# Second layer's first 18 chunks gathered from a table without its last two blocks, those two added by counted products

## The chip, the cores and the metric

The kernel runs on one core of one Trainium2 chip. The metric is device time in microseconds (us) of one execution; a kernel's time is the median of its runs. TensorE is called PE here, VectorE DVE, ScalarE ACT, GpSimd POOL and SyncE SP, as the profile does. POOL and SP also issue transfers (DMAs); an indirect DMA of POOL, a gather, fetches 128 rows of a table by 128 row numbers.

## The reference, cut to what matters

The kernel computes two layers of a graph network over 6250 nodes of 512 numbers and 100,000 edges, which come sorted by `dst`.

```python
norm = -dinv[src] * dinv[dst]                    # dinv: 1/sqrt(degree by src)

def cheb_conv(x, W0, W1, b):
    tx1 = segment_sum(x[src] * norm[:, None], dst, num_segments=N)
    return x @ W0 + tx1 @ W1 + b

h = maximum(layernorm(x), 0)
h = cheb_conv(h, W1_0, W1_1, b1)
h = layer_norm(h) * gamma + beta
h = where(h >= 0, h, 0.01 * h)
out = x + cheb_conv(h, W2_0, W2_1, b2)
```

Both layers need, for each edge, the row of its source node, added up at its target node. The second layer's rows are the first layer's output.

## The kernel before

**Units of work.** The nodes are cut into 49 blocks of 128 rows (the last has 106), the edges into 782 chunks of 128. Three chunks make a unit, four units a group: 66 groups, the first of which has one unit (chunks 0 to 2), so that group 1 has chunks 3 to 14 and group 2 chunks 15 to 26. Layer 0 and layer 1 (the code counts from 0) run the same loop over the groups, the last loop of `usual_path`.

**Tables.** For each layer a table in DRAM holds the rows that the edges fetch. `tab[0]` is made from `x` at the start. `tab[1]` is written by layer 0, block by block, in `finish` (L565), with a copy of the layer's plain output in `h_tab` (L570).

**Gathers.** `gather_to` issues one indirect DMA on POOL for each chunk (L386): the 128 rows named by column `t` of `sidx` go to one of 57 places in `places`, in a ring, so chunk `t` takes the place that chunk `t - 57` had. A gather waits until PE has used the old chunk; a gather from `tab[1]` also waits for the writes of the rows that it reads. At the top of each group gathers are issued 57 chunks ahead of its first chunk.

**Sums.** `choose` makes on DVE a matrix of zeros and ones for each unit (`sel`, L505), which says which of the unit's 32 target nodes each edge of a chunk belongs to. `sums` multiplies the gathered rows by it (L517), and ACT copies the result to `agg` (L520). `place` moves the groups' sums to the rows of a block by another matrix of zeros and ones, `there` (L530, L532).

**Blocks.** When a block's last group is done, `turn` transposes the block's own rows (L456) and places its sums (L582), and `dense` transposes these (L589), copies them back (`aT`, L591) and makes the products with the two weights (L468). `finish` then does the layer norm on DVE and ACT (L549 to L559), makes the scaled row `t` for `tab[1]` (L562, L563) and `g` for `h_tab` (L567, L568), and SP stores both. The own products of blocks 46, 47 and 48 are made ahead (`EARLY`, tiles `pre`), since these blocks come last. Layer 0's group 64 finishes block 46 ahead of its sums, and blocks 47 and 48 follow after groups 64 and 65.

**Order.** `usual_path` takes the order of PE, POOL and SP from the source (`manual_schedule`). The order of DVE and ACT is made by the scheduler of the framework, which also puts in the waits that the data ask for: a write waits for earlier reads of the same part of a tile. Each engine works through its instructions in order.

**Start of the program.** For its first 60 chunks layer 0 gathers from `x` itself; `look_up` finds the two numbers that each row is scaled with (tiles `is_hi` and `both`, L428 to L435), from group 3 on not any more.

Of the kernel before, what the change touches and what calls it, by code (L numbers as in the profile page):

```python
# [8 lines left out]
F32 = mybir.dt.float32  # L9
BF = mybir.dt.bfloat16  # L10
I32 = mybir.dt.int32
AF = mybir.ActivationFunctionType
OP = mybir.AluOpType
# [6 lines left out]
P = 128  # L20
# [4 lines left out]
Q = 32  # L25
# [2 lines left out]
DRIFT = 32  # L28
RE = 16
RAW = 60  # L30


def parts(r):

    return [(lo, hi) for lo, hi in ((0, r - r % 16), (r - r % 16, r)) if lo < hi]
# [3 lines left out]
def gnn_kernel(  # L39
# [33 lines left out]
    nc = tc.nc  # L73
    N, D = x.shape
    E = src.shape[0]
    NB = -(-N // P)
# [3 lines left out]
    KD = D // P  # L80
    NC = -(-E // P)
# [3 lines left out]
    NS = -(-NU // NQ)  # L85
    unit = [max(0, NU - NQ * (NS - g)) for g in range(NS + 1)]
    rows = [min(P, N - i * P) for i in range(NB)]
    LAST = 8

    const = ctx.enter_context(tc.tile_pool(name="const", bufs=1))  # L90
    dram = ctx.enter_context(tc.tile_pool(name="dram", bufs=1, space=bass.MemoryType.DRAM))
# [2 lines left out]

        return bass.AP(tensor=ap.tensor, offset=ap.offset, ap=[[0, n], [1, ap.shape[0]]])

    tab = [dram.tile([n, D], F32, name=f"tab{i}") for i, n in enumerate((NB * P, N))]
    h_tab = dram.tile([N, D], F32, name="h_tab")

    ident = const.tile([P, P], F32, name="ident")  # L100
    iota_r = const.tile([P, P], F32, name="iota_r")
# [14 lines left out]
    gam = const.tile([P, D], F32, name="gam")  # L116
    bet = const.tile([P, D], F32, name="bet")
    sidx = const.tile([P, NG * P], I32, name="sidx")
    w_sb = [const.tile([P, KD, D], F32, name=f"w{i}") for i in range(2)]
    diff = const.tile([P, P], F32, name="diff")  # L120
    sc = const.tile([P, 2, NB], F32, name="sc")
    pick = const.tile([P, P], BF, name="pick")
    src_lo = const.tile([P, P], BF, name="src_lo")
    src_hi = const.tile([P, RAW], F32, name="src_hi")
    p_id = const.tile([P, 1], F32, name="p_id")
# [4 lines left out]
    places = stay.enter_context(tc.tile_pool(name="places", bufs=1)).tile([P, NB + RE, D], F32, name="places")  # L130
    w_at = NB - 2 * KD
    order = list(range(NB, NB + RE)) + list(range(w_at))
# [31 lines left out]
    groups, i = [], 0  # L164
# [4 lines left out]
    xs = []  # L169
# [11 lines left out]
        xs.append(t)  # L181
    for t, w in zip(w_sb, (W1_1, W1_0)):
        nc.sync.dma_start(t, w.rearrange("(k p) d -> p k d", p=P))
    for t, v in ((bias1, b1), (bias2, b2), (gam, gamma), (bet, beta)):
        nc.sync.dma_start(t, dup(v, P))

# [166 lines left out]
def usual_path(tc, have):  # L353
    nc = tc.nc
    (x, out, tab, h_tab, ndinv, sidx, dlx, iota_r, w_sb, W2_1, W2_0, w_late, ident, eps, ones, first, nodes_ps, node_of, minus,
     unsorted, ln, dinv, sdinv, bias1, bias2, gam, bet, unseen, unit, N, E, D, NB, NC, NU, NS, KD, rows, places, order,
     groups, xs, sc, pick, src_lo, src_hi, p_id) = (
        have[n] for n in ("x out tab h_tab ndinv sidx dlx iota_r w_sb W2_1 W2_0 w_late ident eps ones first nodes_ps node_of "
                          "minus unsorted ln dinv sdinv bias1 bias2 gam bet unseen unit N E D NB NC NU NS KD rows places "
                          "order groups xs sc pick src_lo src_hi p_id").split())  # L360
    AHEAD = 2
    EARLY = {NB - 3: NS - 11, NB - 2: NS - 9, NB - 1: NS - 7}
    ACT = mybir.EngineType.Activation
# [9 lines left out]
    with ExitStack() as es:  # L373
# [1 line left out]
        psum = es.enter_context(tc.tile_pool(name="main_ps", bufs=2, space=bass.MemoryType.PSUM))  # L375
        es.enter_context(tc.manual_schedule(engines={PE, POOL, SP}))
        is_lo, found, looked, gathered = [], 0, 0, RE
        own_h, own_x, agg, placed, started, pre = {}, {}, {}, {}, {}, {}

        def zr(t):  # L380
            return places[:, order[t % R], :]

        def gather_to(layer, end):
            nonlocal gathered
            for t in range(gathered, min(end, NC)):
                nc.gpsimd.indirect_dma_start(  # L386
                    out=zr(t), out_offset=None, in_=x if layer == 0 and t < RAW else tab[layer],
                    in_offset=bass.IndirectOffsetOnAxis(ap=sidx[:, t : t + 1], axis=0))
            gathered = max(gathered, min(end, NC))

        def make_table(g, engines):

# [24 lines left out]
        def look_up(tag):  # L417
            nonlocal looked
            if looked == RAW:
                return  # L420
            at_lo = psum.tile([P, 4, P], F32, name=tag)
            at = looked
            assert at + 4 <= gathered
            where = is_lo.pop(0)
            for j in range(4):
                nc.tensor.matmul(at_lo[:, j, : 2 * NB], where[:, j, :], sc.rearrange("p k b -> p (k b)"),  # L426
                                 start=True, stop=True)
            is_hi = pool.tile([P, 4, NB], F32, name="is_hi", bufs=1)  # L428
            nc.vector.tensor_tensor(is_hi, src_hi[:, at : at + 4, None].to_broadcast([P, 4, NB]),
                                    iota_r[:, None, :NB].to_broadcast([P, 4, NB]), op=OP.is_equal)  # L430
            both = pool.tile([P, 4, 2, NB], F32, name="both", bufs=1)
            nc.vector.tensor_tensor(both, at_lo[:, :, : 2 * NB].rearrange("p j (k b) -> p j k b", k=2),
                                    is_hi[:, :, None, :].to_broadcast([P, 4, 2, NB]), op=OP.mult)
            ac = pool.tile([P, 4, 2], F32, name="ac", bufs=4)
            nc.vector.tensor_reduce(ac, both, AX.X, OP.add)  # L435
            for j in range(4):
                nc.scalar.activation(zr(at + j), zr(at + j), AF.Relu, bias=ac[:, j, 1:2], scale=ac[:, j, 0:1])
            looked += 4
# [32 lines left out]
        def load_early(layer, i):  # L471
            load_h(layer, i, "pre", len(EARLY))
            pre[i] = own_h[i]
            if layer == 1:
                load_x(i)

# [29 lines left out]
                                            node[:, q : q + k, None, :].to_broadcast([P, k, w, Q]), op=OP.is_equal)  # L506
            return sel, chunk

        def sums(g, sel, chunk):

            n = len(chunk)
            ps = psum.tile([P, D], F32, name="ps")
            todo = [(s, q) for s in range(STEP) for q in range(n) if s < len(chunk[q])]
            if g == NS - 1:
                todo.sort(key=lambda t: chunk[t[1]][t[0]])
            for s, q in todo:
                nc.tensor.matmul(ps[q * Q : (q + 1) * Q, :], sel[:, q, s, :], zr(chunk[q][s]), start=(s == 0),  # L517
                                 stop=(s == len(chunk[q]) - 1))
            agg[g] = pool.tile([P, D], F32, name="agg", bufs=3)
            nc.scalar.activation(agg[g][: n * Q], ps[: n * Q], AF.Copy)  # L520

# [13 lines left out]
        def finish(layer, i, v):  # L535
            r = rows[i]
            v = v[:r]
            if layer == 1:
                o = pool.tile([P, D], F32, name="t")
                if i in EARLY:  # L540
                    nc.vector.tensor_add(o[:r], v, pre.pop(i)[:r])
                else:
                    nc.vector.tensor_add(v, v, bias2[:r])  # L543
                    nc.vector.tensor_add(o[:r], v, own_x.pop(i)[:r])
                for lo, hi in parts(r):
                    nc.sync.dma_start(out[i * P + lo : i * P + hi, :], o[lo:hi])
                return
            if i < NB - 1:
                nc.vector.tensor_add(v, v, pre.pop(i)[:r] if i in EARLY else bias1[:r])  # L549
            st = pool.tile([P, 6], F32, name="st")  # L550
            mv = pool.tile([P, 2], F32, name="mv")
            nc.vector.bn_stats(st[:r], v)
            nc.vector.bn_aggr(mv[:r], st[:r])
            sd = pool.tile([P, 1], F32, name="sd")
            nc.scalar.activation(sd[:r], mv[:r, 1:2], AF.Sqrt, bias=eps[:r])
            rs = pool.tile([P, 1], F32, name="rs")
            nc.vector.scalar_tensor_tensor(v, v, mv[:r, 0:1], gam[:r], op0=OP.subtract, op1=OP.mult)
            nc.vector.reciprocal(rs[:r], sd[:r])
            nc.vector.scalar_tensor_tensor(v, v, rs[:r], bet[:r], op0=OP.mult, op1=OP.add)  # L559

            t = pool.tile([P, D], F32, name="t")
            nc.scalar.activation(t[:r], v, AF.Copy, scale=sdinv[:r, i : i + 1])  # L562
            nc.vector.scalar_tensor_tensor(t[:r], v, dinv[:r, i : i + 1], t[:r], op0=OP.mult, op1=OP.max)  # L563
            for lo, hi in parts(r):
                nc.sync.dma_start(tab[1][i * P + lo : i * P + hi, :], t[lo:hi])  # L565
            g = pool.tile([P, D], F32, name="g", bufs=1)
            nc.scalar.activation(g[:r], v, AF.Copy, scale=SLOPE)  # L567
            nc.vector.tensor_tensor(g[:r], v, g[:r], op=OP.max)  # L568
            for lo, hi in parts(r):
                nc.sync.dma_start(h_tab[i * P + lo : i * P + hi, :], g[lo:hi])  # L570
# [86 lines left out]

        for layer in range(2):
            if layer == 1:
                gathered = 0  # L660
                for i in range(AHEAD):
                    load(layer, i)
            i = 0
            for g in range(NS):
# [16 lines left out]
                if g == NS - 2:  # L681
                    for k, (hT, an) in due:
                        dense(layer, k, hT, an)
                    due = []
                sums(g, *(chosen if g == NS - 1 else choose(g)))
                if layer == 0:
                    if g == 0:
                        more_tables(1, [DVE, ACT])
# [350 lines left out]
```

## Time and profile before

| | |
|---|---|
| median of 3 runs | 2095.71 us (2095.39 to 2096.01) |
| the profiled execution | 2097.45 us |
| its span, from the first to the last instruction | 2095.5 us |
| PE matmul busy | 1742.9 us, 83% of the span |
| POOL busy | 1497.7 us, 71% |
| DVE busy | 673.7 us, 32% |
| ACT busy | 444.6 us, 21% |
| DMA | 520.33 MB, mean 248 GB/s |
| mean granted clock of PE | 0.916 of full speed |

Busy time leaves out the time in which an engine issues: POOL is busy for some 0.95 us of each gather and idle for 0.30 us between two. In the timelines below a row is: start in us from the span's start, length in us, engine, line, operation, what is written and from what, how many instructions are merged in the row, and in brackets the idle time before it and what ended that. A row of the waits is: engine, tile and line that waited, for whom, us in total, times, longest.

### The profile page before, as it was taken

To read this page: it belongs to the slowest core of one execution; us is meant where nothing else is said; L and a number is where in the kernel's file an instruction comes from. 1 tells how busy PE (TensorE), PEld (TensorE's weight loads), DVE (VectorE), ACT (ScalarE), POOL (GpSimd) and SP (SyncE) were. 2 spreads that over 40 slices of the span, in tenths; PEclk is the share of its full clock that TensorE was granted. 3 is DMA by queue.
4 is the path that set the end of the run, shared out by engine and by line. 5 is a ranking of instruction groups with operands and counts; after the bars stand their busy time and mean duration, and the time that the engine had idled before them with its cause. 6 is when DMAs were issued, how large, how long until landed. Compare 5 with 4: busy or idle time off the path is not lost.

```text
span 2095.5 us, 19192 instructions
## 1 busy us (share of the span) xinstructions
PE 1742.9 (83%) x6708; PEld 662.6 (32%) x6708; DVE 673.7 (32%) x1373; ACT 444.6 (21%) x795; POOL 1497.7 (71%) x1577
## 2 busy tenths in 40 slices
PE   5568888988888889889866888988888889888997
PEld 4433323332323233323321323333223233333332
DVE  8983333333243333333340212222112112221221
ACT  8684222222122221222210101101011011010110
POOL 5067777777777777777747777777777777777774
PEclk9779989999999999989997999999999999999999
DMA  9298888787788887878757788878787788788875
GB/s 369 73 364 269 255 255 253 242 256 244 251 281 254 255 247 248 256 246 262 238 183 216 242 253 255 253 244 254 241 255 240 256 255 251 244 256 251 273 236 156
DMA packets 184793, 520.33 MB, mean 248 GB/s; under 512 B 30321, under 2 KB 31883, under 8 KB 184686
## 3 DMA queue, kind: packets, MB, share of 16 engines
q0 software_dynamic: 125120, 410.09, 64.4%
q1 hardware_dynamic: 59566, 108.91, 14.1%
q8 instruction: 55, 0.90, 0.2%
q14 instruction: 52, 0.43, 0.1%
HBM read 467.64 MB, written 51.25 MB: 248 GB/s over the span
## 4 chain that ended last, share of the span: by engine, by line
PE 40%; DMA 33%; POOL 12%; issue 9%; DVE 5%; ACT 1%; POOLq 0%; SPq 0%; ACTq 0%; DVEq 0%
DMA places<-tab,sidx 32%; PE u_ps L468 19%; POOL places L386 12%; PE ps L517 12%; PE an_ps L532 5%; PE hT_ps L589 2%; PE hT_ps L456 1%; DVE lo L254 1%; DVE hi L254 1%; PE both_ps L260 1%; PE hT_ps L426 0%; DVE places L397 0%; DVE places L398 0%; DMA h<-in_x_dram 0%; DMA places<-in_x_dram,sidx 0%
## 5 line engine op out<-in xcount | busy, mean ns | idle before, releaser
L386 POOL DMA_INDIRECT places<-tab,sidx x1504 | 1422.7, 946 | 480.7 <-issue 310.5
L517 PE MATMUL ps<-places,sel 128*32 128x512 f32 x3128 | 630.3, 706 | 256.8 <-DMA places<-tab,sidx 249.9
L517 PEld LDWEIGHTS ps<-places,sel 128*32 128x32 f32 x3128 | 116.9, 118 | 730.7 <-DMA places<-tab,sidx 506.8
L505 DVE TENSOR_TENSOR sel<-dlx,nodes_ps 128x384 f32<-128x384 f32 (+3 forms) x134 | 72.3, 541 | 656.3 <-PE ps L517 656.3
L532 PE MATMUL an_ps<-agg,there 128*128 128x512 f32 (+1 forms) x580 | 267.7, 596 | 1.5 <-ACT agg L520 1.5
L520 ACT ACTIVATE agg<-ps 128x512 f32<-128x512 f32 (+1 forms) x132 | 78.8, 597 | 809.2 <-PE ps L517 807.3
L468 PE MATMUL u_ps<-places,hT 128*128 128x512 f32 (+1 forms) x392 | 180.3, 603 | 2.2 <-ACT hT L458 2.2
L468 PE MATMUL u_ps<-w,hT 128*128 128x512 f32 (+1 forms) x392 | 178.6, 599 | 2.4 <-ACT hT L458 2.4
L468 PE MATMUL u_ps<-places,aT 128*128 128x512 f32 (+1 forms) x392 | 176.5, 593 | 2.3 <-DVE aT L591 2.3
L468 PE MATMUL u_ps<-w,aT 128*128 128x512 f32 (+1 forms) x392 | 176.5, 593 | 2.3 <-DVE aT L591 2.3
L532 PEld LDWEIGHTS an_ps<-agg,there 128*128 128x128 f32 (+1 forms) x580 | 103.2, 191 | 99.3 <-issue 88.2
L458 ACT ACTIVATE hT<-hT_ps 128x512 f32<-128x512 f32 (+1 forms) x98 | 58.2, 594 | 344.6 <-PE hT_ps L456 343.0
L543 DVE TENSOR_TENSOR u_ps<-u_ps,bias 128x512 f32<-128x512 f32 x46 | 32.2, 700 | 278.4 <-PE u_ps L468 278.4
L549 DVE TENSOR_TENSOR u_ps<-u_ps,bias 128x512 f32<-128x512 f32 x46 | 32.2, 700 | 260.1 <-PE u_ps L468 260.1
L530 DVE TENSOR_SCALAR there<-iota_r,node_of 128x128 f32<-128x128 f32 (+1 forms) x290 | 89.0, 307 | 75.8 <-PE an_ps L532 75.5
L386 POOL DMA_INDIRECT places<-in_x_dram,sidx x44 | 44.5, 1011 | 83.9 <-ACT places L400 58.2
L468 PEld LDWEIGHTS u_ps<-w,aT 128*128 128x128 f32 (+1 forms) x392 | 74.1, 190 | 95.4 <-issue 92.4
L468 PEld LDWEIGHTS u_ps<-places,aT 128*128 128x128 f32 (+1 forms) x392 | 74.1, 190 | 95.4 <-issue 92.4
L468 PEld LDWEIGHTS u_ps<-places,hT 128*128 128x128 f32 (+1 forms) x392 | 72.4, 195 | 75.5 <-issue 72.7
L582 ACT ACTIVATE an<-an_ps,ndinv 128x512 f32<-128x512 f32 (+1 forms) x98 | 67.3, 687 | 135.0 <-PE an_ps L532 135.0
L468 PEld LDWEIGHTS u_ps<-w,hT 128*128 128x128 f32 (+1 forms) x392 | 71.3, 192 | 74.7 <-issue 71.7
L591 DVE COPY aT<-hT_ps 128x512 f32<-128x512 f32 (+1 forms) x98 | 67.5, 688 | 37.9 <-PE hT_ps L589 36.2
(138 smaller groups left out, 1089.1 us busy)
## 6 DMA issues: line engine op xcount, KB each, us to landing
places<-tab,sidx POOLq DMA_INDIRECT x1504, 3.8
tab<-t SPq DMA_DIRECT2D x48, 256.0 KB, 3.9
h_tab<-g SPq DMA_DIRECT2D x48, 256.0 KB, 5.5
xt<-in_x_dram SPq DMA_DIRECT2D x48, 256.0 KB, 4.5
out_dram<-t SPq DMA_DIRECT2D x48, 256.0 KB, 4.2
h<-in_x_dram SPq DMA_DIRECT2D x46, 256.0 KB, 5.7
h<-h_tab SPq DMA_DIRECT2D x46, 256.0 KB, 4.5
tab<-places SPq DMA_DIRECT2D x5, 1792.0 KB
```

Of the source, the lines that this page charges most:

```text
L254: nc.vector.tensor_tensor(t, s[:, g * 2 * GJ : (g + 1) * 2 * GJ].rearrange("p (j s) -> p j s", s=2)[:, :, None, :] .to_broadcast([EP, GJ, ...
L386: nc.gpsimd.indirect_dma_start(out=zr(t), out_offset=None, in_=x if layer == 0 and t < RAW else tab[layer], in_offset=bass.IndirectOffsetO ...
L458: nc.scalar.activation(hT[:, :, :r], ps[:, :, :r], AF.Copy)
L468: nc.tensor.matmul(u_ps[:r], hT[:, kc, :r], w[:, kc, :], start=(start and kc == 0), stop=(stop and kc == KD - 1))
L505: nc.vector.tensor_tensor(sel[:, q : q + k, :w, :], of, node[:, q : q + k, None, :].to_broadcast([P, k, w, Q]), op=OP.is_equal)
L517: nc.tensor.matmul(ps[q * Q : (q + 1) * Q, :], sel[:, q, s, :], zr(chunk[q][s]), start=(s == 0), stop=(s == len(chunk[q]) - 1))
L520: nc.scalar.activation(agg[g][: n * Q], ps[: n * Q], AF.Copy)
L530: nc.vector.tensor_scalar(there[:m, :r], iota_r[:m, :r], node_of[:m, g : g + 1], -(1.0 + i * P), op0=OP.subtract, op1=OP.is_equal)
L532: nc.tensor.matmul(placed[i][:r], there[:m, :r], agg[g][:m, :], start=(g == inside[i][0]), stop=(g == inside[i][-1]))
L582: nc.scalar.activation(an[:r], placed.pop(i)[:r], AF.Copy, scale=ndinv[:r, i : i + 1])
L589: nc.tensor.transpose(ps[:, kc, :r], an[:r, kc * P : (kc + 1) * P], ident[:r, :r])
L591: nc.vector.tensor_copy(aT[:, :, :r], ps[:, :, :r])
```

## The change

Layer 1's chunks 0 to 17 are no longer gathered with the others but by `gather_ahead`, which layer 0's group 64 calls when block 46 is finished (`LATE = 2` blocks, `AHEAD_OF = 18` chunks). They read only `tab[1][: zero_row + 1]`, blocks 0 to 46 and one more row, `zero_row` = 47 x 128 = 6016, which holds zeros. Edges whose source is in block 47 or 48 read that zero row: `eidx` is the smaller of the source's number and 6016. Blocks 47 and 48 are stored one row further down in `tab[1]`, and `shift` adds 1 to the row numbers from 6016 on in `sidx`, in two halves: columns 0 to 511 in layer 0's group 50, columns 512 to 781 in layer 1's group 2. Layer 1's other gathers start at chunk 18 and read `sidx` as before.

What the zero row left out is added in groups 0 to 2 of layer 1. `count_late` counts on PE, for each of the two blocks, how many edges go from each of its rows to each of a unit's 32 target nodes: for each chunk and block DVE makes a mask (edge by row of the block), and PE multiplies it by `sel`. `sums` then multiplies these counts by the rows of the two blocks, which stay in SBUF: for blocks 47 and 48 `finish` writes `t` into the block's `pre` tile (`late`). That makes 36 masks, 36 matmuls of counts and 12 products of 512 columns.

To make room in SBUF, `is_hi` and `both` of `look_up` now lie in the buffers of `aT` and `g`.

```diff
+LATE = 2
+AHEAD_OF = 18
...
-    tab = [dram.tile([n, D], F32, name=f"tab{i}") for i, n in enumerate((NB * P, N))]
+    tab = [dram.tile([n, D], F32, name=f"tab{i}") for i, n in enumerate((NB * P, N + 1))]
+    zero_row = (NB - LATE) * P
...
+    eidx = const.tile([P, AHEAD_OF], I32, name="eidx")
+    e_src = const.tile([P, AHEAD_OF], F32, name="e_src")
...
+    nc.sync.dma_start(tab[1][zero_row : zero_row + 1, :], places[P - 1 : P, NB - 1, :])
...
+        def gather_ahead():
+
+            for t in range(AHEAD_OF):
+                nc.gpsimd.indirect_dma_start(
+                    out=zr(t), out_offset=None, in_=tab[1][: zero_row + 1, :],
+                    in_offset=bass.IndirectOffsetOnAxis(ap=eidx[:, t : t + 1], axis=0))
+
+        def shift(lo, hi):
+
+            at, up = (pool.tile([P, D], F32, name="xt")[:, : hi - lo] for _ in range(2))
+            nc.vector.tensor_copy(at, sidx[:, lo:hi])
+            if lo == 0:
+                nc.vector.tensor_copy(e_src, at[:, :AHEAD_OF])
+                nc.vector.tensor_scalar_min(up[:, :AHEAD_OF], at[:, :AHEAD_OF], float(zero_row))
+                nc.vector.tensor_copy(eidx, up[:, :AHEAD_OF])
+            nc.vector.tensor_single_scalar(up, at, float(zero_row), op=OP.is_ge)
+            nc.vector.tensor_add(at, at, up)
+            nc.vector.tensor_copy(sidx[:, lo:hi], at)
...
-            is_hi = pool.tile([P, 4, NB], F32, name="is_hi", bufs=1)
+            is_hi = pool.tile([P, KD, P], F32, name="aT", bufs=1)[:, :, :NB]
...
-            both = pool.tile([P, 4, 2, NB], F32, name="both", bufs=1)
+            both = pool.tile([P, D], F32, name="g", bufs=1)[:, : 8 * NB].rearrange("p (j k b) -> p j k b", j=4, k=2)
...
             pre[i] = own_h[i]
+            if layer == 0 and i >= NB - LATE:
+                late[i] = pre[i]
...
+        def count_late(sel, chunk):
+
+            some = [q for q, c in enumerate(chunk) if c[0] < AHEAD_OF]
+            if not some:
+                return None
+            ps = psum.tile([P, LATE, P], F32, name="hT_ps")
+            for q in some:
+                for b in range(LATE):
+                    for k, t in enumerate(chunk[q]):
+                        hot = pool.tile([P, P], F32, name="there", bufs=3)
+                        nc.vector.tensor_scalar(hot, iota_r, e_src[:, t : t + 1], -float(zero_row + b * P),
+                                                op0=OP.subtract, op1=OP.is_equal)
+                        nc.tensor.matmul(ps[:, b, q * Q : (q + 1) * Q], hot, sel[:, q, k, :], start=(k == 0),
+                                         stop=(k == len(chunk[q]) - 1))
+            cnt = pool.tile([P, LATE, P], F32, name="cnt", bufs=1)
+            w = len(some) * Q
+            nc.vector.tensor_copy(cnt[:, :, :w], ps[:, :, :w])
+            return cnt
...
-        def sums(g, sel, chunk):
+        def sums(g, sel, chunk, cnt=None):
...
-                                 stop=(s == len(chunk[q]) - 1))
+                                 stop=(s == len(chunk[q]) - 1 and (cnt is None or chunk[q][0] >= AHEAD_OF)))
+            for b in range(LATE if cnt is not None else 0):
+                r = rows[NB - LATE + b]
+                for q in range(n):
+                    if chunk[q][0] < AHEAD_OF:
+                        nc.tensor.matmul(ps[q * Q : (q + 1) * Q, :], cnt[:r, b, q * Q : (q + 1) * Q],
+                                         late[NB - LATE + b][:r], start=False, stop=(b == LATE - 1))
...
-            t = pool.tile([P, D], F32, name="t")
+            t = late[i] if i in late else pool.tile([P, D], F32, name="t")
...
+            at = i * P + (i in late)
             for lo, hi in parts(r):
-                nc.sync.dma_start(tab[1][i * P + lo : i * P + hi, :], t[lo:hi])
+                nc.sync.dma_start(tab[1][at + lo : at + hi, :], t[lo:hi])
...
             if layer == 1:
-                gathered = 0
+                gathered = AHEAD_OF
...
                     due = []
-                sums(g, *(chosen if g == NS - 1 else choose(g)))
+                    if layer == 0:
+                        assert i == NB - LATE and gathered == NC
+                        gather_ahead()
+                sel, chunk = chosen if g == NS - 1 else choose(g)
+                sums(g, sel, chunk, count_late(sel, chunk) if layer == 1 else None)
+                if g == (NS - 16, 2)[layer]:
+                    shift(*((0, SHIFTED), (SHIFTED, NC))[layer])
```

## The prediction, made before the changed kernel had run

> **What bounds the kernel now.** I read the totals first, then who GpSimd (POOL) waited for, then the timelines around the change of layer, one engine at a time. POOL sends one gather per chunk of 128 edges (L386). Its waits over the whole span, and its timeline where layer 0 ends:
>
> ```profile
> POOL places L386 <- issue: 315.0, 1034, 0.3
> POOL places L386 <- DMA h_tab<-g: 22.8, 1, 22.8
> ...
> 1069.82 0.94 POOL L386 DMA_INDIRECT places<-tab,sidx  x1 [0.30 <-issue]
> 1071.07 0.95 POOL L386 DMA_INDIRECT places<-tab,sidx  x1 [0.30 <-issue]
> 1094.77 0.94 POOL L386 DMA_INDIRECT places<-tab,sidx  x1 [22.75 <-DMA h_tab<-g]
> 1096.01 0.95 POOL L386 DMA_INDIRECT places<-tab,sidx  x1 [0.30 <-issue]
> ```
>
> The reader is to see 0.95 us of work and 0.30 us of idle per gather: a beat of 1.25 us, always "issue", so nothing holds POOL. Layer 1 is 782 beats from 1094.77 to 2071.22, and a fixed tail follows to 2095.5. Only one long wait breaks the beat: 22.75 us in which layer 1's first gather waits for the last table rows. Who writes those rows is on SyncE's queue:
>
> ```profile
> 1060.13 0.32 SPq L565 DMA_DIRECT2D tab<-t  x1
> ...
> 1068.07 0.32 SPq L565 DMA_DIRECT2D tab<-t  x1
> ...
> 1081.28 0.32 SPq L565 DMA_DIRECT2D tab<-t  x1
> ...
> 1091.67 0.73 SPq L565 DMA_DIRECT2D tab<-t  x2
> ```
>
> These are blocks 45, 46, 47 and 48; the last one's issue at 1091.67 lets POOL go 3.1 us later. TensorE (PE) is not the bound: between 691 and 1033 us it waits for gathers 40.9 us in total.
>
> **What I expect of each part.** In its aim the change is sound: 18 of the 782 beats (22.5 us) need only blocks 0 to 46 and fit the hole. But `shift` writes new indices into `sidx`, which the gathers read. A write of columns 0 to 511 must wait until layer 0's gather 511 has landed, one of columns 512 to 781 until its last, gather 781, has. PE, POOL and SP run in the order of the source; VectorE (DVE) and ScalarE have theirs from the scheduler. In the changed program as built the first write-back stands between L559 and L563 of block 26, and the second, which the source has in layer 1's group 2, between L563 and L568 of layer 0's block 43. In the trace of before these two places are
>
> ```profile
> 684.18 0.86 DVE L559 SCALAR_TENSOR_TENSOR u_ps<-u_ps,rs,bet 128x512 f32<-128x512 f32 x1
> 684.95 0.27 DVE L530 TENSOR_SCALAR there<-iota_r,node_of 128x128 f32<-128x128 f32 x1
> 685.80 0.75 DVE L563 SCALAR_TENSOR_TENSOR t<-u_ps,dinv,t 128x512 f32<-128x512 f32 x1 [0.57 <-ACT t L562]
> ...
> 1019.55 0.28 DVE L530 TENSOR_SCALAR there<-iota_r,node_of 128x128 f32<-128x128 f32 x1
> 1020.30 0.69 DVE L568 TENSOR_TENSOR g<-u_ps,g 128x512 f32<-128x512 f32 x1 [0.47 <-ACT g L567]
> ```
>
> and the gathers waited for are issued at 733.46 (270 beats before the last) and 1071.07. With the median landing of 3.8 us they are there at 737.3 and 1074.9: VectorE would stand still for 52 us and again for up to 55 us. That a waiting instruction holds all behind it is visible in the trace:
>
> ```profile
> 1078.02 0.69 ACT L562 ACTIVATE t<-u_ps,sdinv 128x512 f32<-128x512 f32 x1 [1.29 <-DVE u_ps L559]
> ...
> 1080.03 0.55 DVE L505 TENSOR_TENSOR sel<-dlx,nodes_ps 128x384 f32<-128x384 f32 x1 [2.05 <-PE ps L517]
> 1080.51 0.75 DVE L563 SCALAR_TENSOR_TENSOR t<-u_ps,dinv,t 128x512 f32<-128x512 f32 x1
> ```
>
> L563's input is ready at 1078.71, yet it runs only behind L505, which waits for PE. The Trainium skill says the same, and it speaks against this change (TensorE: Matmul & The Clock Gate, "Architectural detail: the array is 16× 32×32, not 1× 128×128": VectorE and ScalarE are strict first-in first-out). By that rule alone the two waits are unavoidable; the row agrees with 1.8 us lost.
>
> **First stall, 685 to 737.** Behind it stand block 26's `t` and block 27's `aT`. PE stops at 690.96 ahead of block 27's second products. VectorE then needs about 0.9 us for the write-back and one step of the other half, and 2.7 us from L563 to the end of `aT` (685.80 to 688.50), so PE resumes at 740.9, 50 us late. POOL goes on as long as the ring of 57 places lasts: gather 528 takes chunk 471's place at 754.7; PE reaches chunk 471 after 8 products (3.6, and 1.2 for a cold clock, below), transposes 0.4 and placing 2.7, at 748.9. So 5.8 us are to spare, the next needs (gather 540 at 769.7) leave more, and I cost this stall at nothing. PE's 40.9 us of waits until 1033 take up most of the 50; some 10 remain, inside the second stall. With the cover gone each microsecond POOL waits for a place is one at the end.
>
> **Second stall.** It ends at 1074.9 whatever the backlog. Then VectorE does the write-back (128x270; between the 0.27 of a 128x128 and the 0.69 of a 128x512 row, taken 0.4), L568, one L530, L505 and L591 at their spacing in the trace (0.6, 0.2, 0.5, 0.69): PE goes on at 1077.3 with block 44's second products. Before:
>
> ```profile
> 1036.62 3.60 PE L468 MATMUL u_ps<-w,aT 128*128 128x512 f32 x8
> ...
> 1043.16 2.78 PE L517 MATMUL ps<-places,sel 128*32 128x512 f32 x22
> 1046.20 1.04 PE L517 MATMUL ps<-places,sel 128*32 128x512 f32 x2 [0.27 <-DMA places<-tab,sidx]
> ...
> 1165.61 4.76 PE L468 MATMUL u_ps<-places,hT 128*128 128x512 f32 x8
> ```
>
> That is 40.7 us later. Two corrections: after idle time eight products took 4.76 instead of 3.60 (+1.2; none would be the lower end), and group 63's sums (4.0 us, waiting for chunks) take 2.7, since all chunks are there (-1.3). The Trainium skill (same page, "What's actually happening") has PE at half clock for about 3.4 us after an idle window; that would make it 1.7, the sum 0.5 more. Net 40.6.
>
> **The sum.** Block 46's rows leave at 1068.07 + 40.6 = 1108.7 and land 3.1 later: the 18 early gathers run from 1111.8 to 1134.3. Block 48: between its L552 and L563 three counting masks and then a copy and three more masks are put on VectorE (0.25 each apart); they fill its wait for ScalarE and add about 1.1. Its rows leave at 1091.67 + 40.6 + 1.1 = 1133.4 and, now beside gathers, take the median 3.9: gather 18 starts at 1137.3. Before, gather 18 started at 1094.77 + 22.5 = 1117.3. So POOL is **20.0 us late** from there on; 764 beats and the tail are as before.
>
> **Costed at nothing.** The 36 masks (0.30 each, L530), 36 count matmuls (0.25 to 0.5: two weight loads of 0.12 to 0.19 and a short pass each) and 12 products: 22 to 32 us on two engines side by side, 19 at worst in a row on PE, under PE's seven waits for first chunks between 1087 and 1130 (25 us in the trace), with the ring's 57 places behind; uncovered up to 19. The reading steps of `shift` (some 5 us) lie in VectorE's waits for PE (333 us from 400 to 1000). The zero row is one 2 KB store on SP near 45 us, when SP next has work at 94.47. `is_hi` and `both` in the places of `aT` and `g` add waits only among VectorE's own instructions in their old order. `late` only keeps tiles that nothing loads into before layer 1's group 53.
>
> The profiled execution took 2097.45 us, 1.95 around its span of 2095.5; the median of the runs shown is 2095.71. 20.0 on each: span 2115.5, median 2115.7.
>
> **Rivals.**
> 1. *The stalls don't bite and the aim is reached* (faster). It needs VectorE to come to the second write-back after 1074.9, thus a backlog of 55 us at 1020; I find 10. Then the early gathers run 1072.3 to 1094.8, gather 18 starts at 1094.77 + 1.1 + 0.8 = 1096.7, 20.6 early: 2075.1. For it: the hole is real. Against: the two places in VectorE's order. 0.06.
> 2. *The first stall also empties the ring.* With PE at half clock throughout, group 40's first matmul is at 754.4 (in time) but group 41's at 774.6 against 769.7: 4.9 more, carried to the end, 2121. For it: the granted clock was 0.60 in the 10 us after the gap at the change of layer. 0.12.
> 3. *Counted products on the path*, half of the 19 uncovered: 2125. Against: 25 us of waits there. 0.08.
> 4. *The early gathers wait for blocks 47 and 48 after all*, so nothing is early: gather 0 at 1137.3, 42.5 late, 2138. Against: they read rows up to 6016 and block 47 starts at 6017. 0.03.
>
> The forecast has 0.70, and 0.01 is left for no change. About 0.2% (4 us) is what a measurement of this kernel can tell. Faster 0.06, same 0.02, slower 0.92. Range: down to 2108, where PE resumes warm and rows land quickly (1.2, 0.8, 1.1 less, and some 4 for landing times and steps); up to 2128, taking in rivals 2 and 3.
>
> **What would show it.** Right: two gaps of about 50 us on VectorE ending at landings of gathers, near 737 and 1075, with `sidx` written right behind; PE idle about 1048 to 1077; POOL's beat unbroken up to 1071, then a wait of about 40 us, 18 gathers, a wait of a few us. Wrong: VectorE busy through 1020 to 1075, POOL breaking its beat near 755 to 785, or gathers of layer 1 waiting for PE.

## The result, and the profile after

The changed kernel takes **2120.17 us** (median of 4 runs, 2116.97 to 2121.44), the kernel before, beside it, 2095.86 us (4 runs). The ratio is 1.0113, 95% interval 1.0095 to 1.013: 24 us slower. The profiled execution took 2120.7 us with a span of 2118.9 us, 23.4 us more than the span before. GpSimd is busy for 1497.6 us, as before (1497.7), TensorE for 1722.4 us, which is 20.5 us less, and VectorE for 685.4 us, 11.7 us more but only a third of the span. So the time is not in longer computation but in waits.

First GpSimd's waits, in the same columns as those shown of before (L394 is the old L386, L402 the early gather):

```profile
POOL places L394 <- issue: 320.1, 1050, 0.5
...
POOL places L402 <- DVE aT L646: 41.7, 1, 41.7
```

Then its timeline where layer 0 ends:

```profile
1070.37 0.95 POOL L394 DMA_INDIRECT places<-tab,sidx  x1 [0.30 <-issue]
1113.00 0.94 POOL L402 DMA_INDIRECT places<-tab,eidx  x1 [41.68 <-DVE aT L646]
...
1134.24 0.94 POOL L402 DMA_INDIRECT places<-tab,eidx  x1 [0.30 <-issue]
1138.62 0.94 POOL L394 DMA_INDIRECT places<-tab,sidx  x1 [3.44 <-DVE there L548]
```

The 18 early gathers do run without the last two blocks. But the hole of 22.75 us that they were to fill is now 41.68 us and lies ahead of them, with a further 3.44 us behind. Chunk 18 is gathered at 1138.62; before, it came 18 beats after 1094.77, at 1117.27. That is 21.35 us of the loss. The name "DVE aT L646" does not say what ended the 41.68 us. It is VectorE's copy for block 47, which ended 0.36 us ahead of the gather and is no input of it. In e10_first_on_pool (below) the same wait names no engine, and among the semaphores that the gather waits for in its trace is none of VectorE. The two rows, the first from the changed kernel, the second from e10_first_on_pool:

```profile
1111.95 0.69 DVE L646 COPY aT<-hT_ps 128x512 f32<-128x512 f32 x1 [0.55 <-PE hT_ps L644]
...
1112.89 0.95 POOL L402 DMA_INDIRECT places<-tab,eidx  x1 [41.70 <-issue]
```

What the gather needs last by the source is a store of table rows on SyncE's queue:

```profile
1109.88 0.32 SPq L620 DMA_DIRECT2D tab<-t  x1
...
1123.10 0.32 SPq L620 DMA_DIRECT2D tab<-pre  x1
...
1133.65 0.72 SPq L620 DMA_DIRECT2D tab<-pre  x2
```

Blocks 46, 47 and 48 leave at 1109.88, 1123.10 and 1133.65. The first early gather starts 3.1 us behind block 46 (in e10_first_on_pool 3.1 as well, and before 3.1 behind block 48), chunk 18's gather 5.0 us behind block 48. All three blocks are some 42 us later than before (block 46: 1068.07). VectorE's timeline shows why (L416 is the write-back into `sidx`):

```profile
684.61 0.44 DVE L584 TENSOR_SCALAR there<-iota_r,node_of 128x128 f32<-128x128 f32 x1
736.73 0.43 DVE L416 CAST sidx<-xt 128x512 int32<-128x512 f32 x1 [51.68 <-DMA places<-tab,sidx]
...
737.56 0.73 DVE L617 SCALAR_TENSOR_TENSOR t<-u_ps,dinv,t 128x512 f32<-128x512 f32 x1
...
1018.93 0.28 DVE L584 TENSOR_SCALAR there<-iota_r,node_of 128x128 f32<-128x128 f32 x1
1074.96 0.30 DVE L416 CAST sidx<-xt 128x270 int32<-128x270 f32 x1 [55.75 <-DMA places<-tab,sidx]
1075.17 0.68 DVE L623 TENSOR_TENSOR g<-u_ps,g 128x512 f32<-128x512 f32 x1
...
1076.43 0.68 DVE L646 COPY aT<-hT_ps 128x512 f32<-128x512 f32 x1
```

Twice VectorE stands still, for 51.68 and 55.75 us, and each time until a gather has landed ("DMA places<-tab,sidx"): the write of new row numbers waits for the last gather that reads the old ones, gather 511, issued at 732.82, and gather 781, issued at 1070.37. Block work with its inputs ready (L617, L623) stands behind it. TensorE's timeline around both places:

```profile
740.30 5.65 PE L495 MATMUL u_ps<-w,aT 128*128 128x512 f32 x8 [49.30 <-DVE aT L646]
...
748.89 2.78 PE L565 MATMUL ps<-places,sel 128*32 128x512 f32 x24
...
1032.59 3.60 PE L495 MATMUL u_ps<-w,hT 128*128 128x512 f32 x8
...
1077.17 6.16 PE L495 MATMUL u_ps<-w,aT 128*128 128x512 f32 x8 [40.99 <-DVE aT L646]
...
2106.45 5.22 PE L495 MATMUL u_ps<-places,aT 128*106 128x512 f32 x8 [0.69 <-DVE aT L646]
```

After the first stop of 49.30 us TensorE has caught up: its products at 1032.59 stand where they stood before (1033.18). Between 691 and 1033 us its waits for gathers fell from 40.9 to 17.6 us, and the 552 instructions of its sums (L565, before L517) counted as busy for 83.4 us in place of 112.1. After the second, of 40.99 us, there is nothing left to catch up in, because layer 1 cannot start before the last blocks are written.

### The profile page after: what moved, and what is told of

Same layout as the page of the kernel before. It is cut to its first block, busy times and chain, and to the rows that moved or that the text cites. A ratio compares the mean times of both kernels' runs of the same rounds, so it can differ in the third digit from the quotient of the medians.

```text
span 2118.9 us, 19441 instructions
## 1 busy us (share of the span) xinstructions
PE 1722.4 (81%) x6804; PEld 674.6 (32%) x6804; DVE 685.4 (32%) x1423; ACT 445.5 (21%) x795; POOL 1497.6 (71%) x1577
## 4 chain that ended last, share of the span: by engine, by line
PE 41%; DMA 32%; POOL 12%; issue 9%; DVE 4%; ACT 1%; POOLq 0%; SPq 0%; DVEq 0%; ACTq 0%
DMA places<-tab,sidx 31%; PE u_ps L495 19%; PE ps L565 12%; POOL places L394 11%; PE an_ps L586 5%; PE hT_ps L644 2%; PE hT_ps L483 1%; DVE lo L261 1%; DVE hi L261 1%; PE both_ps L267 1%; DMA h<-in_x_dram 1%; PE hT_ps L550 0%; PE hT_ps L453 0%; DVE places L424 0%; DMA places<-in_x_dram,sidx 0%
## 5 line engine op out<-in xcount | busy, mean ns | idle before, releaser
L394 POOL DMA_INDIRECT places<-tab,sidx x1486 | 1405.5, 946 | 455.8 <-issue 315.0
L565 PE MATMUL ps<-places,sel 128*32 128x512 f32 x3128 | 583.0, 680 | 209.4 <-DMA places<-tab,sidx 203.2
L565 PEld LDWEIGHTS ps<-places,sel 128*32 128x32 f32 x3128 | 112.2, 117 | 642.2 <-DMA places<-tab,sidx 428.8
L495 PE MATMUL u_ps<-w,aT 128*128 128x512 f32 (+1 forms) x392 | 181.1, 606 | 92.5 <-DVE aT L646 92.5
L495 PE MATMUL u_ps<-places,hT 128*128 128x512 f32 (+1 forms) x392 | 184.7, 616 | 2.2 <-ACT hT L485 2.2
L394 POOL DMA_INDIRECT places<-in_x_dram,sidx x44 | 44.5, 1011 | 83.3 <-ACT places L427 59.0
L644 PE MATMUL hT_ps<-ident,an 128*128 128x128 f32 x392 | 68.5, 301 | 14.2 <-ACT an L637 14.2
```

Of the source, the lines that this page charges most:

```text
L394: nc.gpsimd.indirect_dma_start(out=zr(t), out_offset=None, in_=x if layer == 0 and t < RAW else tab[layer], in_offset=bass.IndirectOffsetO ...
L495: nc.tensor.matmul(u_ps[:r], hT[:, kc, :r], w[:, kc, :], start=(start and kc == 0), stop=(stop and kc == KD - 1))
L644: nc.tensor.transpose(ps[:, kc, :r], an[:r, kc * P : (kc + 1) * P], ident[:r, :r])
```

## The experiments

Ten kernels ran. Each ratio is against the kernel before on the same chip.

### Four kernels on a chip that could not tell

Four kernels ran first on a chip on which the kernel before took 2507.89 us (14 runs), with a granted clock near 0.84 and short gaps on all engines. They ran again on two other chips, three as e5_stall_only, e6_own_tile and e7_both_gone (there the kernel before took 2098.48 us), the fourth as e10_first_on_pool (2099.28 us, the chip of e8_no_counts and e9_not_early too); their edits are shown there.

> The kernel before, and nothing of the change but the second write-back: in layer 1's group 2 VectorE copies columns 512 to 781 of sidx to a tile and back unchanged. As built the copy back stands at the same place as in the changed kernel, between L563 and L568 of layer 0's block 43, with the same eight waits for gathers. Stall theory: VectorE stands still from about 1020 to 1075, block 48's rows leave some 41.8 us later (in the changed kernel 1133.65 against 1091.67, less the masks), all 782 gathers of layer 1 start that much later since none is early: 2095.9 + 41.8 = 2137.7 us. Rival, that the counted products and masks make the changed kernel slower: two small copies, 2096 to 2097 us.

> The changed kernel, but the second half's new indices go to a tile of their own (sidx_late, read by layer 1's gathers from chunk 512 on), so that this write waits for no gather. The first write-back and its stall from 685 to 737 stay, and so do the masks, counts and products. Stall theory: the whole gain appears; block 48's rows leave at 1091.67 + 1.1, land 5.0 later, gather 18 starts at 1097.8 instead of 1117.3: 19.5 us less than before, 2076 to 2079 us. Rival, counted products: still 2118 to 2121 us. Rival, the first stall costs what it measures (50 us on TensorE, some of it left at the end): 2085 to 2100 us.

> The changed kernel, but the first write-back is done by GpSimd, whose order is that of the source, so that the first stall is gone; the second write-back stays where it was on VectorE. Stall theory with the first stall free: the same as the changed kernel, 2118 to 2122 us, with one or two us more if GpSimd's own copy costs a beat. If the first stall cost its part of the 24 us: 2100 to 2115 us.

> The changed kernel with the first write-back on GpSimd and the second half in a tile of its own: neither stall is left. Stall theory: as e2_own_tile, 2076 to 2079 us, plus one to two us for GpSimd's copy. If the first stall costs something, this is faster than e2_own_tile by it. Rival, counted products: 2118 to 2121 us.

Measured: e1_stall_only 2504.23 us (0.9986, 0.9964 to 1.0008); e2_own_tile 2497.92 us (0.994, 0.9917 to 0.9963); e3_first_on_pool 2491.78 us (0.9923, 0.9905 to 0.9942); e4_both_gone 2494.49 us (0.9931, 0.9906 to 0.9955). None is what either theory expected. GpSimd's waits in e2_own_tile say why:

```profile
POOL places L395 <- remote: 218.2, 84, 4.7
POOL places L395 <- PE ps L574: 117.7, 34, 16.0
...
POOL places L405 <- DVE aT L655: 47.1, 1, 47.1
```

There GpSimd waits 117.7 us for TensorE to free places (15.5 us in e7_both_gone on another chip, where none was longer than 0.3), and the early gathers wait 47.1 us at the change of layer although the second write-back no longer holds VectorE: TensorE is behind for another reason. In e1_stall_only GpSimd waits 103.4 us for it in the same way. That the stall alone (e1_stall_only) costs nothing there fits with it, since it then stands in time that is lost anyway; no run tested that reading. On the question of the study, where GpSimd's beat sets the pace, these four are inconclusive.

### e5_stall_only: the second stall alone, in the kernel before

The same kernel as e1_stall_only. Nothing of the change but a copy of columns 512 to 781 out of `sidx` and back, in layer 1's group 2:

```diff
                 sums(g, *(chosen if g == NS - 1 else choose(g)))
+                if layer == 1 and g == 2:
+                    at = pool.tile([P, D], F32, name="xt")[:, : NC - D]
+                    nc.vector.tensor_copy(at, sidx[:, D:NC])
+                    nc.vector.tensor_copy(sidx[:, D:NC], at)
```

> Again the kernel before with nothing of the change but the second write-back (columns 512 to 781 of sidx copied to a tile and back unchanged), on another chip: in the first run of it every engine lost time to gaps that no other engine ended, and the kernel before took 2508 us there. Where the kernel before takes about 2096 us: stall theory 2137.7 us (block 48's rows 41.8 us later, all 782 gathers of layer 1 with them). Rival, counted products: 2096 to 2097 us.

Measured: 2138.51 us (2136.57 to 2141.04), ratio 1.0194 (1.0177 to 1.0211). Two short copies cost 40.0 us. From the timeline, two rows of VectorE and layer 1's first gather on GpSimd:

```profile
1020.04 0.46 DVE L530 TENSOR_SCALAR there<-iota_r,node_of 128x128 f32<-128x128 f32 x1
1075.11 0.30 DVE L689 CAST sidx<-xt 128x270 int32<-128x270 f32 x1 [54.60 <-DMA places<-tab,sidx]
...
1136.64 0.94 POOL L386 DMA_INDIRECT places<-tab,sidx  x1 [64.94 <-DMA h_tab<-g]
```

A copy that the source puts behind the sums of layer 1's group 2 runs at 1075.11, before layer 1 has gathered one row, and VectorE idles for 54.60 us between its row of 1020.04 and the copy. Gather 0 starts 41.87 us later than before (1094.77), where 41.8 was expected. So the stall's price is shown by itself, and shown to be larger than the whole loss of the change.

### e6_own_tile: the second half into a tile of its own

The same kernel as e2_own_tile: layer 1's gathers from chunk 512 on read a tile that nothing reads earlier, so its write waits for no gather.

```diff
+        sidx_late = pool.tile([P, NC - SHIFTED], I32, name="sidx_late", bufs=1)
...
-                    in_offset=bass.IndirectOffsetOnAxis(ap=sidx[:, t : t + 1], axis=0))
+                    in_offset=bass.IndirectOffsetOnAxis(
+                        ap=sidx_late[:, t - SHIFTED : t - SHIFTED + 1] if layer and t >= SHIFTED else sidx[:, t : t + 1],
+                        axis=0))
...
+            if lo > 0:
+                at = pool.tile([P, D], F32, name="xt")[:, : hi - lo]
+                nc.vector.tensor_copy(at, sidx[:, lo:hi])
+                nc.vector.scalar_tensor_tensor(at, at, float(zero_row), at, op0=OP.is_ge, op1=OP.add)
+                nc.vector.tensor_copy(sidx_late, at)
+                return
```

> Again the changed kernel with the second half's new indices in a tile of their own; the first write-back and its stall stay. Where the kernel before takes about 2096 us: stall theory 2076 to 2079 us; counted products as the cause 2118 to 2121 us; a first stall that costs at the end 2085 to 2100 us.

Measured: 2077.72 us (2076.06 to 2081.21), ratio 0.9913 (0.9895 to 0.9931). From the timeline, a row of VectorE (the first stall, which is still there) and GpSimd's at the change of layer:

```profile
736.63 0.43 DVE L425 CAST sidx<-xt 128x512 int32<-128x512 f32 x1 [52.02 <-DMA places<-tab,sidx]
...
1070.51 0.95 POOL L395 DMA_INDIRECT places<-tab,sidx  x1 [0.30 <-issue]
1072.57 0.94 POOL L405 DMA_INDIRECT places<-tab,eidx  x1 [1.11 <-DMA h_tab<-g]
...
1093.89 0.95 POOL L405 DMA_INDIRECT places<-tab,eidx  x1 [0.30 <-PE ps L580]
1095.86 0.94 POOL L395 DMA_INDIRECT places<-tab,sidx  x1 [1.02 <-PE hT_ps L559]
```

The beat now goes almost unbroken from one layer into the next: waits of 1.11 and 1.02 us in place of 22.75. Chunk 18 is gathered at 1095.86, 21.4 us earlier than before, and the time falls by 20.8 us, with the counted products, the masks and the first stall of 52.02 us all in place.

### e7_both_gone: the first write-back off VectorE as well

The same kernel as e4_both_gone: e6_own_tile, and in `shift`

```diff
-            nc.vector.tensor_copy(sidx[:, lo:hi], at)
+            nc.gpsimd.tensor_copy(sidx[:, lo:hi], at)
```

> Again the changed kernel with neither stall (first write-back on GpSimd, second half in its own tile). Where the kernel before takes about 2096 us: stall theory as e6_own_tile, 2076 to 2079 us, plus one to two us for GpSimd's copy; if the first stall costs something, faster than e6_own_tile by it; counted products as the cause 2118 to 2121 us.

Measured: 2076.32 us (2075.45 to 2076.83), ratio 0.9899 (0.9883 to 0.9916), **the fastest version of the study**, ahead of both kernels. GpSimd's queue has the layer-0 gathers in order, so the copy comes to its turn, 0.63 us at 904.2, when gather 511 is long done; the one or two us expected for it do not show. Against e6_own_tile it is 1.4 us less, with intervals that overlap: the first stall is worth nothing that these runs can tell.

### e8_no_counts: e7_both_gone without masks, counts and counted products

```diff
-                sums(g, sel, chunk, count_late(sel, chunk) if layer == 1 else None)
+                sums(g, sel, chunk, None)
```

> As e7_both_gone, but leaves out the masks, the counts and the 12 products, so that the rows of blocks 47 and 48 are missing from the sums of groups 0 to 2 of layer 1. What the counted products cost once no stall is left: if they are hidden but for the masks in block 48's layer norm, gather 18 starts about 1.1 us earlier and the time is 2075 us against 2076.3; if they hold TensorE and with it the end, 5 to 19 us less, 2057 to 2071 us.

Measured: 2080.6 us (2079.44 to 2081.6), ratio 0.9909 (0.9893 to 0.9926). Leaving 36 masks, 36 matmuls and 12 products out gains nothing: the ratio is not below that of e7_both_gone (0.9899), and by the ends of the two intervals at most some 5 us can be uncovered. The few tenths that they might cost cannot be read from this run, on another chip than e7_both_gone: chunk 18 is gathered at 1099.35, 2.8 us later than there and not 1.1 earlier. Part of that is in one row of TensorE. First TensorE's row for block 48's eight products in e7_both_gone:

```profile
1083.82 3.68 PE L504 MATMUL u_ps<-w,aT 128*106 128x512 f32 x8 [0.69 <-DVE aT L655]
```

and the same row in e8_no_counts:

```profile
1084.54 5.29 PE L504 MATMUL u_ps<-w,aT 128*106 128x512 f32 x8 [0.69 <-DVE aT L655]
```

The same work after the same idle time took 1.61 us longer, at a granted clock of 0.70 (1084.5 to 1090) where e7_both_gone had 1.00 (1083.8 to 1089). The last section says where that comes from.

### e9_not_early: e7_both_gone with the 18 gathers not early

The 18 gathers are issued at the start of layer 1 and read the whole table, so they wait for block 48 as the others do. All else of the change stays.

```diff
-        def gather_ahead():
+        def gather_ahead(table):
...
-                    out=zr(t), out_offset=None, in_=tab[1][: zero_row + 1, :],
+                    out=zr(t), out_offset=None, in_=table,
...
+                gather_ahead(tab[1])
...
-                        gather_ahead()
+                        pass
```

> As e7_both_gone, but the 18 gathers are issued at the start of layer 1 and read the whole table's place, so they wait for block 48 as before; zero row, shift, counts and products stay. If the early gathers are the whole gain, it is gone: gather 0 at about 1096.5 instead of 1094.8, 2097 to 2099 us where the kernel before takes 2096 to 2098. If part of the gain came from elsewhere: between 2076 and 2095 us.

Measured: 2100.51 us (10 runs, 2097.4 to 2102.88), ratio 1.0008 (0.9998 to 1.0018). The gain of e7_both_gone is gone, and the hole is back in GpSimd's timeline:

```profile
1093.41 0.94 POOL L405 DMA_INDIRECT places<-tab,eidx  x1 [22.74 <-DMA h_tab<-g]
```

So the early gathers are the gain, and everything else that the change adds costs 1.2 us in the medians, between nothing and 4 us by the interval. Gather 0 starts at 1093.41 and not at the expected 1096.5: it follows block 48's store (1090.28) by 3.1 us, as before.

### e10_first_on_pool: the first stall taken away, the second left

The changed kernel with the first write-back on GpSimd (the edit of e7_both_gone), the second still on VectorE into `sidx`, its sum made in one instruction as in e6_own_tile. The same kernel as e3_first_on_pool.

> Again the changed kernel with the first write-back on GpSimd and the second on VectorE as it was. If the first stall is free: as the changed kernel, 2117 to 2121 us. If it costs its part: 2100 to 2115 us.

Measured: 2121.51 us (2120.88 to 2122.27), ratio 1.0107 (1.009 to 1.0124); the changed kernel has 1.0113. From the timeline, a row of VectorE and one of GpSimd:

```profile
1074.64 0.30 DVE L412 CAST sidx<-xt 128x270 int32<-128x270 f32 x1 [55.73 <-DMA places<-tab,sidx]
...
1138.13 0.94 POOL L394 DMA_INDIRECT places<-tab,sidx  x1 [3.02 <-PE hT_ps L556]
```

With the 52 us of the first stall gone, the second ends where it ended (1074.64 against 1074.96) and chunk 18 is gathered 0.5 us earlier. This is the other half of e6_own_tile: the first stall costs nothing that can be told, whether the second is there or not.

## Why the prediction was right

The forecast was 2115.7 us in a range of 2108 to 2128; the median is 2120.17. The mechanism was the forecast one, and the sum was 4.5 us short: 1.4 us up to chunk 18 and 2.1 in the tail, by the profiled executions, and 1.1 in how these lie to the medians of the runs. Point by point:

- **Two stalls on VectorE, from write-backs that the scheduler put far ahead of their place in the source.** Forecast to end with landings at 737.3 and 1074.9; they ended at 736.7 and 1075.0. e5_stall_only shows the second with nothing else of the change in the kernel. The Trainium skill has VectorE as strict first-in first-out (TensorE: Matmul & The Clock Gate, "Architectural detail: the array is 16× 32×32, not 1× 128×128"); the trace agrees, with 51.68 and 55.75 us in which ready work stood behind the write.
- **The first costs nothing.** Forecast: TensorE resumes at 740.9 and begins chunk 471 at 748.9, 5.8 us before GpSimd needs its place. It resumed at 740.3 and began at 748.9. That this is the very time forecast is luck: it resumed 0.6 us earlier, and its eight products took 0.9 us more than the 4.8 forecast. GpSimd's beat is unbroken at gather 528:

```profile
754.06 0.95 POOL L394 DMA_INDIRECT places<-tab,sidx  x1 [0.30 <-issue]
```

  The backlog of 10 us that I left for 1033 was none, so that TensorE stood idle from 1036 and not from 1048. The 40.9 us of waits had shown only part of its slack; 28.7 us more lay in sums that counted as busy. That changed no number, since the second stall sets its own end. e10_first_on_pool and the pair e6_own_tile, e7_both_gone show the zero.
- **The second is worth 40.6 us on block 46.** Its rows left 41.8 us later than before. The term that was mis-sized is the cold clock: eight products took 6.16 us and not 3.60, 2.56 more where I took 1.2 from a row of 4.76. The granted clock shows why. The columns are: stretch and its length, TensorE's busy time (rows), granted clock, DMA share, GB/s; first the changed kernel, then the kernel before, around the row of 4.76:

```profile
1078.75:1082.17 3.42, 3.42 (x5) 0.50 0.00 0
1082.17:1085.58 3.41, 3.41 (x12) 1.00 0.00 0
...
1164.54:1167.95 3.41, 3.41 (x8) 0.50 0.78 261
1167.95:1171.37 3.42, 3.42 (x9) 1.00 0.75 217
```

  The clock had gone to half during the stop and stayed there until 1082.17, 5.00 us into the products that began at 1077.17; that cost 2.5. The row of 4.76 began at 1165.61 in the middle of a stretch at half clock and had only 2.34 us of it, which cost 1.2. So that row could not stand for a start after a long stop. The rows after 41 to 49 us of idle give 2.05 (the 5.65 at 740.30), 2.56 and 2.80 (6.40, in e10_first_on_pool). By the 3.4 us at half clock that the Trainium skill states (TensorE: Matmul & The Clock Gate, "What's actually happening") it would be 1.7, an estimate, nearer and still short.
- **The masks' 1.1 us ahead of block 48** were 0.2. From block 46's store to block 48's it is 23.77 us with the change (and in e6_own_tile 23.76), 23.60 before and in e5_stall_only, where block 46 was late but nothing was counted.
- **Block 48's landing beside gathers**, put at 3.9 us, took 4.97 us. The cold clock's 1.4 too little, the masks' 0.9 too much, the landing's 1.1 too little and 0.2 of small steps too much make 1.4: gather 18 came 21.35 us late and not 20.0. That these misses offset each other is luck.
- **The tail as before** was not quite: from chunk 18's gather to the end it took 980.3 us where it had taken 978.2. Of these 2.1 us, 1.54 are the last eight products, 5.22 us and not 3.68, at a granted clock of 0.72 and not 1.00. That the change brings this is not shown: the same rows come out at either length among the experiments (last section).
- **Costed at nothing.** e6_own_tile contains the masks, the counts, the products, the zero row, the reads of `shift` and the new places of `is_hi` and `both`, and gains 20.8 us; e9_not_early contains them too and stands at 1.0008.

The rivals. The first, stalls that don't bite, was put at 2075.1 us, and that is about what is reached once the second stall is taken away (e7_both_gone, 2076.32 on a chip where the kernel before took 2098.48). The second, an empty ring, is excluded by the beat above. The third, counted products on the path, is excluded by e6_own_tile, where the beat of layer 1 is unbroken from chunk 18 to the last with all of them in place, and e8_no_counts agrees. The fourth, early gathers that wait for the last blocks, is excluded by their start 3.1 us behind block 46's store and 20.7 us ahead of block 48's. The chances listed add up to 0.93 for slower and 0.01 for no change, where the forecast says 0.92 and 0.02; nothing hangs on it.

## What to carry to other kernels

A write into a tile that many transfers still read is not ordered by where it stands in the source but by the last reader, and a scheduler that puts such a write early turns it into a stop of the whole in-order engine: look for it in the built order of the engine, not in the diff, and give the new values a tile of their own. What a stop costs is set by the slack behind it: 52 us in the middle of a layer cost nothing here, and 55 us ahead of a change of layer cost 40, because there the next stage waits for the last result. And a name behind "<-" in a wait need not be the releaser: the same wait was put down to "DVE aT" in one run (41.68 us) and to "issue" in another (41.70), and each time it ended 3.1 us behind a store, so follow what the instruction needs by the source. Last, a cost read from a row holds only for the state that the row began in: the 4.76 us began in the middle of a stretch at half clock, and a start after a stop cost twice as much.

## What the runs showed of the hardware

- The same eight products after the same 0.69 us of idle time came out at 3.68 us or at 5.2 to 5.4 us. They took longer at the end of the changed kernel (5.22), of e5_stall_only (5.38) and of e9_not_early (5.17) and in layer 0's block 48 of e8_no_counts (5.29), and took 3.68 at the end of the kernel before and of the four other experiments. No idle time in the 10 us ahead was over 0.8 us, and the rows there were the same in the two pairs compared (the changed kernel and the kernel before, e8_no_counts and e7_both_gone). What differs is where the steps of the granted clock lie.
- In the clock records of the changed kernel, the kernel before and e5 to e10 the granted clock is 1.00 or 0.50, and all its changes lie whole multiples of 3.41 us apart. Of its 403 falls from 100 us on, 393 follow a step of 3.41 us in which TensorE was busy for less than half; 41 of 434 steps of that kind were followed by none, so half is not a sharp limit. At the end of the changed kernel the step from 2102.76 to 2106.17 has TensorE busy for 1.69 us, and the clock is 0.50 until 2109.58. In the kernel before the same rows are cut otherwise, into steps with 2.10 and 2.51 us busy (2079.31 to 2082.72 and on to 2086.13), and the clock stays at 1.00. The Trainium skill has the half clock come after an idle window of some 3.4 us (TensorE: Matmul & The Clock Gate, "What's actually happening"). The traces agree with that length, and show that a window in which no single idle time is over 0.8 us can bring it.
- A store of block 48's rows in two parts was followed by the gather that waits for it after 3.1 us where no other gather was under way (the kernel before, e5_stall_only, e9_not_early), and after 4.6 to 5.0 us where others were (the changed kernel 4.97, e6_own_tile 4.8, e7_both_gone 4.7, e8_no_counts 4.8, e10_first_on_pool 4.6).
- One chip ran the kernel before 20% slower than the others (2507.89 us against 2095.86 to 2099.28), with the ratios of four edits moved by up to 2.1% (e1_stall_only 0.9986, e5_stall_only 1.0194, one and the same kernel). What slowed it was not found.
